# One eighth of the holographic attention of seven chunks is computed in the expert stage

## The chip, the cores and the metric

The kernel runs on one core of a Trainium2 chip. The metric is device microseconds (us) of one execution. The kernel before takes 1104.69 us (median of three runs, 1103.02 to 1106.05). A core has engines that run side by side, each through its own queue in order: PE (matrix products, results into PSUM), DVE (elementwise work, reductions, scans), ACT (elementwise functions), POOL (elementwise work), SP (here: issuing DMA transfers).

## The reference, cut to what matters

Two transformer-like layers over x of shape (16, 256, 128), float32. Every sublayer is x = x + gate * f(normalized and modulated x).

```python
x = x + ga * _L0_attn_ref(h, ...)       # layer 0: attention, 16 heads of 8
x = x + gb * _L0_ffn_ref(h, ...)        # layer 0: 16 experts, the best 4 of each token
x = x + ga * _L1_attn_ref(h, ...)       # layer 1: holographic attention
x = x + gb * _L1_ffn_ref(h, ...)        # layer 1: mixing of each token with the one before
```

The part that the change touches is the holographic attention; H * D = 16 * 64 = 1024 features:

```python
def _holo_fused_step(v, binder, probe):
    mem = jnp.cumsum(v * binder, axis=1)
    return jnp.real(mem * probe) / scale        # scale: sqrt(t + 1)
k = jnp.exp(1j * (k_real * PHASE_SCALE))
rotors = jnp.exp(1j * (t[:, None, None] * freqs))[None]
out_pos = _holo_fused_step(v, rotors, jnp.conj(rotors))
out_assoc = _holo_fused_step(v, jnp.conj(k_shifted), k)   # k_shifted: k one token later
out = out_pos * g_pos + out_assoc * g_assoc
return out.reshape(Bb, Tt, HD) @ Wo
```

So for every feature there are two running sums over the 256 tokens ("pos", bound by the rotor, and "assoc", bound by the phasor of the token before), each of a cosine and a sine; each sum is multiplied by its probe, and all go through Wo.

## The kernel before, in words

The 16 batch rows are worked on in 8 chunks of two rows (512 tokens). Three stages follow one another: the attention of layer 0; the expert stage; the holographic stage, which also holds the mixing of layer 1.

*Expert stage* (`for n in range(total + 4)`, 128 steps n = 16 c + e: chunk c, expert e). Step n: `gate_up(n)` has PE write pg (L752) and pup (L754), DVE add bias and limit into g (L756), ACT make u from pup (L758) and silu back into pg (L759), POOL clamp u (L760). `act(n - 1)` has DVE multiply u by pg (L766) and POOL by the scores of the expert (L767, tile `wide`). `down(n - 3)` has PE add the expert's product to the chunk's accumulator acc (L775; at e = 0 after a product with the biases b_dn, L774). pg has three PSUM banks, pup two, acc two; one bank (p_m) serves all else. `wide` comes by DMA, four experts (1 MB) at a time, into three buffers. At e = 2 ACT evicts the accumulator of the chunk before (chunk_end1, L784), at e = 3 it is transposed (pmo) and DVE adds it to x (L794); at e = 5 DVE takes the figures of the norm (L177, L178), at e = 7 POOL finishes them.

Side work is cut into small steps by generators, one step of each generator a step n: `last_end` (from n = 1) finishes layer 0's attention of the last batch row, and then lets `route` choose experts for the last five chunks (DVE, L261 to L285); its scores are due at n = 39. `prepare` (from n = 33) makes the modulation of layer 1, the rotor's angles and its sines (`turn_rotor`), scaled weights, the tokens of chunk 0 and, in `first_steps`, the values and phasors of the first two holographic parts and the bound values of the first.

*Holographic stage* (`for n in range(last + 2)`). The 1024 features are 8 parts of 128 (j), so 64 parts (c, j). Per part n: PE projects keys and values pk, pv of part n + 2 (L1035, L1039); DVE runs two scans of 128x1024 (cosine and sine, two rows of 256; `summed`, L1072): assoc into SBUF, pos into PSUM; `phases` (L1051, off) and the probe's product m_pos (L1298) are DVE's too; ACT makes the phasor (L1057 to L1059); POOL multiplies the assoc sums by their probe (L1303) and binds the values of part n + 1 twice (`binders`, L1069); PE takes four products of 512 columns through Wo (`out_project`, L1086). `keep` holds the scan's factors, 1 and 0 at the start of a row. At a chunk's end ACT scales by the gate (oT, L1099), PE transposes (pho), DVE adds to x (`into_stream`, L1112). The mixing of a finished chunk runs in later parts, placed by j: means, figures, power (POOL, L1161, L1162), norm, tokens, two pairs of products (pk2, pr2: `mixed`), values, gating, output. `tokens`, `turned` and `into_tokens` make the normalized tokens of the next chunk. Within the two stages the order on PE, DVE, ACT and POOL is as written.

## Time and profile before

| | us |
|---|---|
| median of three runs | 1104.69 |
| the profiled execution | 1106.3 |
| its span, first to last instruction | 1104.5 |
| attention of layer 0 | 0 to 306 |
| expert stage | 306 to 663.6 |
| holographic stage | 663.6 to 1083.2 |
| last chunk's ending | 1083.2 to 1104.5 |

Busy over the whole span: PE 1041.6, DVE 873.0, ACT 688.1, POOL 810.9. A stretch of the span has its own row of busy times, a group of instructions its mean duration (ns), and a row of the timeline its start and duration; what an engine waited for stands in square brackets behind the operation that it waited with. Spans of the same engine overlap by some hundredths of a microsecond, so that the spacing of starts is a little shorter than the durations.

### The profile page before, as it was taken

Reading aid. Unit: us, or ns where it says so; the run is one execution under the profiler, and the core shown is the slowest. Engines: PE = TensorE matmul, PEld = TensorE weight load, DVE = VectorE, ACT = ScalarE, POOL = GpSimd, SP = SyncE. Lnnn points to the kernel's source line nnn. Section 1 sums busy time; section 2 is a strip of 40 time slices with the busy share of each in tenths; the row PEclk is TensorE's granted clock in tenths of the full one; section 3 lists DMA queues with packets and bytes.
Section 4 is the critical chain, followed back from the end, with each engine's and each line's share of the span. In section 5 each row is a group of like instructions: output and inputs, shape, how many; then the busy total and the mean of one; then the engine's idle time right before and its main releaser. Section 6 shows DMA issues by size and latency. Waiting matters only on the chain.

```text
span 1104.5 us, 15892 instructions
## 1 busy us (share of the span) xinstructions
PE 1041.6 (94%) x5361; PEld 526.3 (48%) x5361; DVE 873.0 (79%) x1283; ACT 688.1 (62%) x1390; POOL 810.9 (73%) x720
## 2 busy tenths in 40 slices
PE   7999999999999999999999998889999999898987
PEld 5566766666644444444444443334443444343433
DVE  6678888997655877655555559999999999999994
ACT  3676767666655455555685445657767676867663
POOL 3245334542567677777776889999999999999992
PEclk8999999999999999999999999999999999999999
DMA  3102100000153223232222210000000000000000
GB/s 114 41 10 64 56 3 3 2 4 3 42 187 115 77 80 113 77 115 90 102 115 79 76 39 0 1 0 0 1 10 1 10 0 10 0 10 0 11 0 28
DMA packets 27200, 46.71 MB, mean 42 GB/s; under 512 B 7504, under 2 KB 22128, under 8 KB 23024
## 3 DMA queue, kind: packets, MB, share of 16 engines
q1 hardware_dynamic: 26576, 45.45, 11.9%
q8 instruction: 42, 0.69, 0.3%
q14 instruction: 38, 0.31, 0.1%
q10 hardware_dynamic: 544, 0.26, 0.1%
HBM read 43.07 MB, written 2.37 MB: 41 GB/s over the span
## 4 chain that ended last, share of the span: by engine, by line
PE 56%; DVE 23%; POOL 12%; issue 4%; ACT 3%; DMA 1%; SPq 0%; DVEq 0%; POOLq 0%; ACTq 0%
PE pg L752 9%; PE acc L775 9%; PE pup L754 9%; DVE sum_assoc L1072 7%; DVE mem L1072 7%; PE s L399 5%; PE po L453 5%; PE st L433 5%; DVE m_pos L1298 4%; POOL sum_assoc L1303 3%; POOL bound_assoc L1069 3%; POOL bound_pos L1069 3%; PE pout L1086 3%; PE pq L526 2%; DVE maxima L411 2%
## 5 line engine op out<-in xcount | busy, mean ns | idle before, releaser
L441 ACT ACTIVATE exp<-st 128x512 f32<-128x512 f32 x256 | 132.2, 602 | 88.2 <-PE st L433 88.2
L411 DVE TENSOR_REDUCE maxima<-s 128x2 f32<-128x512 f32 x256 | 158.9, 684 | 27.0 <-PE s L399 26.8
L767 POOL TENSOR_TENSOR u<-u,wide 128x512 f32<-128x512 f32 x128 | 163.1, 1275 | 19.3 <-DVE u L766 9.0
L756 DVE TENSOR_SCALAR g<-pg,b_gu 128x512 f32<-128x512 f32 x128 | 95.7, 747 | 103.2 <-PE pg L752 102.5
L758 ACT ACTIVATE u<-pup,b_gu 128x512 f32<-128x512 f32 x128 | 87.8, 686 | 138.0 <-PE pup L754 129.0
L1086 PE MATMUL pout<-m_pos,w_pos 128*128 128x512 f32 x256 | 128.7, 626 | 36.1 <-DVE m_pos L1298 28.9
L1072 DVE TENSOR_TENSOR_SCAN sum_assoc<-keep,bound_assoc 128x1024 f32<-128x1024 bf16 x64 | 146.0, 2282 | 4.6 <-POOL bound_assoc L1069 4.3
L1072 DVE TENSOR_TENSOR_SCAN mem<-keep,bound_pos 128x1024 f32<-128x1024 bf16 x64 | 145.4, 2272 | 0.0
L1303 POOL TENSOR_TENSOR sum_assoc<-sum_assoc,phasor 128x1024 f32<-128x1024 f32 x64 | 140.1, 2189 | 0.3 <-DVE sum_assoc L1072 0.3
L1069 POOL TENSOR_TENSOR bound_pos<-v,rotor 128x1024 f32<-128x1024 f32 x63 | 137.9, 2189 | 1.0 <-PE acc L775 1.0
L1069 POOL TENSOR_TENSOR bound_assoc<-v,phasor 128x1024 f32<-128x1024 f32 x63 | 138.0, 2191 | 0.0
L760 POOL TENSOR_SCALAR u<-u 128x512 f32<-128x512 f32 x128 | 81.6, 638 | 72.7 <-ACT u L758 69.2
L775 PE MATMUL acc<-u,w_dn 128*128 128x512 f32 x256 | 131.9, 597 | 2.9 <-POOL u L767 2.8
L752 PE MATMUL pg<-hT,w_gu 128*128 128x512 f32 x256 | 131.5, 595 | 1.6 <-DVE u L766 1.1
L754 PE MATMUL pup<-hT,w_gu 128*128 128x512 f32 x256 | 130.7, 592 | 0.0
L1086 PE MATMUL pout<-sum_assoc,w_assoc 128*128 128x512 f32 x256 | 120.7, 594 | 1.7 <-POOL sum_assoc L1303 1.7
L1086 PEld LDWEIGHTS pout<-m_pos,w_pos 128*128 128x128 f32 x256 | 45.3, 192 | 115.1 <-DVE m_pos L1298 66.5
L766 DVE SCALAR_TENSOR_TENSOR u<-u,pg 128x512 f32<-128x512 f32 x128 | 86.7, 678 | 8.2 <-POOL u L760 6.9
L759 ACT ACTIVATE pg<-g 128x512 f32<-128x512 f32 x128 | 75.9, 593 | 15.9 <-DVE g L756 15.8
L433 PE MATMUL st<-qx,kx 32*128 32x256 f32 x1024 | 82.3, 389 | 1.3 <-DMA qx<-turned 1.2
L1036 ACT ACTIVATE whole<-pk 128x512 f32<-128x512 f32 x62 | 36.9, 595 | 74.9 <-PE pk L1035 74.3
L399 PE MATMUL s<-kx,qx 32*128 32x256 f32 x1024 | 78.1, 409 | 4.1 <-DVE kx L536 1.8
(274 smaller groups left out, 1724.9 us busy)
## 6 DMA issues: line engine op xcount, KB each, us to landing
wide<-scores SPq DMA_DIRECT2D x32, 1024.0 KB
qx<-turned SPq DMA_DIRECT2D x256, 1.0 KB
w_gu<-in_gate_up_dram SPq DMA_DIRECT2D x8, 256.0 KB
out_dram<-x SPq DMA_DIRECT2D x16, 128.0 KB
x<-in_x_dram SPq DMA_DIRECT2D x14, 128.0 KB
w_dn<-in_down_dram SPq DMA_DIRECT2D x4, 256.0 KB
ga<-ga_rows SPq DMA_DIRECT2D x1, 768.0 KB
w_k<-in_Wk_dram SPq DMA_DIRECT2D x1, 512.0 KB
```

The costliest lines, as they stand in the source:

```text
L399: nc.tensor.matmul(s[g][:, i, :], qs[c][r][rows_, k, ts(i, P)], ks[c][rows_, r // NS, k, :], start=True, stop=True,)
L411: nc.vector.tensor_reduce(mx[:, :, g], s[g], AX.X, ALU.max, negate=True)
L433: nc.tensor.matmul(st[g][:, i, :], ks[c][rows_, r // NS, k, ts(i, P)], qs[c][r][rows_, k, :], start=True, stop=True,)
L441: nc.scalar.activation(e[:, g, :, :], st[g], AF.Exp, scale=QSCALE)
L752: nc.tensor.matmul(pg, w_gu[:, e, 0 : 2 * D : 2], h2, start=True, stop=True)
L754: nc.tensor.matmul(pu, w_gu[:, e, 1 : 2 * D : 2], h2, start=True, stop=True)
L767: nc.gpsimd.tensor_tensor(u, u, wide[n // SOME][:, n % SOME, :], ALU.mult)
L775: nc.tensor.matmul(accs[c], w_dn[:, e, :], work.pop(n), start=False, stop=(e == NE - 1))
L1069: nc.gpsimd.tensor_tensor(w[nm], v2, bind, ALU.mult)
L1072: nc.vector.tensor_tensor_scan(dst.rearrange("p s k t -> p (s k t)"), keep.rearrange("p s t -> p (s t)"), work[n][nm].rearrange("p s k t - ...
L1086: nc.tensor.matmul(pos[c], w[:, j, :], m[:, k, :, :].rearrange("p k t -> p (k t)"), start=(j == 0 and i == 0 and k == 0), stop=(j == NJ - ...
L1303: nc.gpsimd.tensor_tensor(m, m, phasor[(n - 1) % 3][:, :, :, 1:], ALU.mult)
```

## The change

Part j = 7 of chunks 0 to 6 leaves the holographic stage (`PARTS`: 7 parts for these chunks, 8 for chunk 7) and is computed by the generator `part_ahead(c)`, one step a step n of the expert stage from e = 8 of chunk c + 1. It makes the chunk's tokens (kept in the tile hT2 of that chunk), pv and pk of this part, and its phasor; then, one a step, eight pieces: two kinds (pos, assoc) of two rows and of cosine and sine, 128x256 each. POOL binds a piece, and a step later DVE reads it: a scan into a PSUM row, the product with probe and gate, and the addition to totals[c]. For chunk 6 there are two pieces a step. In the holographic stage totals[c] goes through one product of PE with w_last, the unscaled last rows of Wo, at j = 1.

Beside that: `prepare` starts at n = 1 in place of 33, with the angles of the last two parts first; `last_end` starts at n = 7 in place of 1; `wide` is loaded for two experts at a time; acc has one PSUM bank in place of two, the other goes to the PSUM row; and the places of the mixing are counted from the end of its chunk (2 to 13 parts later), not by j.

```diff
+AHEAD = NCH - 1
+PARTS = [NJ - 1 if c < AHEAD else NJ for c in range(NCH)]
...
-        SOME = 4
+        SOME = 2
...
-        lp = ctx.enter_context(tc.tile_pool(name="norm1", bufs=2, side="right"))
+        lp = ctx.enter_context(tc.tile_pool(name="norm1", bufs=1, side="right"))
...
+        w_last = load_late("w_last", [P, D], a["Wo"][HD - P :, :])
...
-                for nm, n in (("pe_g", 3), ("pe_u", 2), ("pe_acc", 2), ("pe_m", 1))
+                for nm, n in (("pe_g", 3), ("pe_u", 2), ("pe_acc", 1), ("pe_m", 1))
             )
+            p_sum = scope.enter_context(tc.tile_pool(name="pe_sum", bufs=1, space=bass.MemoryType.PSUM))
...
+            sums = p_sum.tile([P, 2, T], F32, tag="sum", name="sums")
+            nc.vector.memset(sums[:, 0, 0:1], 1.0)
+            keep_all, row = sums[:, 0, 0:1].to_broadcast([P, T]), sums[:, 1, :]
...
+                yield from angles(NJ // 2 - 1)
+                for h in range(2):
+                    nc.scalar.activation(w_k1[:, ts(h, 512)], w_k1[:, ts(h, 512)], AF.Copy, scale=PHASE / TWO_PI)
+                    yield
+                turn_rotor(NJ - 1)
+                yield
+                for p in range(NJ // 2 - 1):
+                    yield from angles(p)
...
-                for h in range(2):
-                    nc.scalar.activation(w_k1[:, ts(h, 512)], w_k1[:, ts(h, 512)], AF.Copy, scale=PHASE / TWO_PI)
-                    yield
...
-                tokens(0)
-                yield
-                pt = turned(0, hns.pop(0), p_m, "a1")
-                yield
-                into_tokens(0, pt)
-                for j in range(NJ):
-                    yield
+                for j in range(NJ - 1):
                     turn_rotor(j)
+                    yield
                 yield from first_steps()
...
+            def part_ahead(c):
+                j = NJ - 1
+                tokens(c)
+                yield
+                yield
+                into_tokens(c, turned(c, hns.pop(c), p_m, "a1"))
+                yield
+                flat = hTs[c].rearrange("p k t -> p (k t)")
+                v = cross.tile([P, 2, T], F32, tag="o", name=f"v_ahead_{c}")
+                pv = p_m.tile([P, 2, T], F32, tag="m", name=f"pv0_{c}")
+                nc.tensor.matmul(pv, w_v1[:, ts(j, P)], flat, start=True, stop=True)
+                nc.scalar.copy(v, pv)
+                bound = {}
+                def bind(nm, k, s, by):
+                    t = cross.tile([P, T], F32, tag=("heads", "y")[s], name=f"bound_ahead_{nm}_{c}_{k}_{s}")
+                    nc.gpsimd.tensor_tensor(t, v[:, k, :], by, ALU.mult)
+                    bound[nm, k, s] = t
+                def read(nm, k, s, i, probe):
+                    dst = totals[c][:, k, :]
+                    nc.vector.tensor_tensor_scan(row, keep_all, bound.pop((nm, k, s)), 0.0, ALU.mult, ALU.add)
+                    first = i == 0 and s == 0
+                    nc.vector.scalar_tensor_tensor(
+                        dst if first else row, row, gates[:, j, i : i + 1], probe, ALU.mult, ALU.mult
+                    )
+                    if not first:
+                        nc.vector.tensor_tensor(dst, row, dst, ALU.add)
+                cs = late.tile([P, 2, 2, T + 1], F32, tag="phasor_ahead", name=f"phasor_ahead_{c}")
+                nc.gpsimd.memset(cs[:, :, :, 0:1], 0.0)
+                pieces = [
+                    ("pos", k, s, 0, rotor[:, j, s, :], rotor[:, j, s, :]) for k in range(2) for s in range(2)
+                ] + [("assoc", k, s, 1, cs[:, s, k, 0:T], cs[:, s, k, 1:]) for k in range(2) for s in range(2)]
+                many = 2 if c == AHEAD - 1 else 1
+                def go(i):
+                    for q in pieces[max(i - 1, 0) * many : i * many]:
+                        read(*q[:4], q[5])
+                    for q in pieces[i * many : (i + 1) * many]:
+                        bind(*q[:3], q[4])
+                for i in range(8 // many + 1):
+                    yield
+                    if i == 0:
+                        pk = p_m.tile([P, 2, T], F32, tag="m", name=f"pk0_{c}")
+                        nc.tensor.matmul(pk, w_k1[:, ts(j, P)], flat, start=True, stop=True)
+                        off = cross.tile([P, 2, T], F32, tag="hn4", name=f"off_ahead_{c}")
+                        nc.scalar.activation(off, pk, AF.Copy, bias=ROUND)
+                        nc.vector.scalar_tensor_tensor(off, off, ROUND, pk, ALU.subtract, ALU.subtract)
+                    if i == 1:
+                        nc.scalar.activation(cs[:, 1, :, 1:], off, AF.Sin, scale=-TWO_PI_IN)
+                        nc.scalar.activation(off, off, AF.Abs)
+                        nc.scalar.activation(cs[:, 0, :, 1:], off, AF.Sin, bias=half_pi, scale=-TWO_PI_IN)
+                    go(i)
...
-                hTs[c] = lp.tile([P, 2, T], F32, tag="hT3", name=f"hT3_{c}")
+                hTs[c] = hT2[c]
...
+            totals = [late.tile([P, 2, T], F32, tag=f"total{c}", name=f"total{c}") for c in range(AHEAD)]
...
-            tasks.append([None, last_end(), 1])
-            def go_on():
-                for t in tasks[:1]:
-                    try:
-                        next(t[1])
-                    except StopIteration:
-                        tasks.remove(t)
+            last_steps = last_end()
...
                     widened(n // SOME + 2)
-                if n >= 1:
-                    go_on()
-                if n > 2 * NE:
+                if n > 6:
+                    next(last_steps, None)
+                if n > 0:
                     next(ready, None)
+                if e == 8 and 1 <= c <= AHEAD:
+                    ahead.append(part_ahead(c - 1))
+                for steps_ in ahead:
+                    next(steps_, None)
                 if n == total:
-                    assert next(ready, None) is None
+                    assert all(next(t, None) is None for t in [ready, last_steps, *ahead])
...
-        steps = [(c, j) for c in range(NCH) for j in range(NJ)]
+        steps = [(c, j) for c in range(NCH) for j in range(PARTS[c])]
...
                     start=(j == 0 and i == 0 and k == 0),
-                    stop=(j == NJ - 1 and i == (n < len(steps) - 1) and k == 1),
+                    stop=(j == PARTS[c] - 1 and i == (n < len(steps) - 1) and k == 1),
+                )
+            if i == 0 and j == 1 and c < AHEAD:
+                nc.tensor.matmul(
+                    pos[c], w_last, totals[c].rearrange("p k t -> p (k t)"), start=False, stop=False
                 )
...
+        begin = [sum(PARTS[:c]) for c in range(NCH)]
         for n in range(last + 2):
-            c, j = divmod(n, NJ)
-            now = c - 1 if 1 <= c <= NCH - 1 and j >= 2 else None
-            mixing = now is not None
-            gone = c - 2 if c >= 2 else None
+            c, j = steps[n] if n <= last else (NCH, 0)
+            place = {n - begin[m + 1]: m for m in (c - 2, c - 1) if 0 <= m < NCH - 1 and n <= last}
...
-            if mixing and j == 7:
-                mixed(now, wk_now, wk_before, "pk2")
-            if gone is not None and j == 0 and n < last:
-                mixed(gone, wr_now, wr_before, "pr2")
-            if gone is not None and j == 1:
-                mix_values(gone)
+            if 7 in place:
+                mixed(place[7], wk_now, wk_before, "pk2")
+            if 8 in place:
+                mixed(place[8], wr_now, wr_before, "pr2")
+            if 9 in place:
+                mix_values(place[9])
             if n + 2 <= last:
...
-            if j in (1, 2) and c:
-                into_stream(2 * (c - 1) + j - 1, pho[:, j - 1])
-            if j == 1 and c + 1 < NCH and n > 1 or n == 2:
+            if j == 1 and c:
+                for k in range(2):
+                    into_stream(2 * (c - 1) + k, pho[:, k])
+            if j == 1 and AHEAD <= c + 1 < NCH:
                 tokens(c + 1)
```

## The prediction

> **What bounds the kernel now.** I first cut the span into its stages, since the shares of the whole mix stages with different limits. Columns: stretch, its length, then busy time of PE, weight loads, DVE, ACT, POOL, then PE clock, DMA share, GB/s.
>
> ```profile
> 663.60:1083.20 419.60, 381.68 (x933) 163.92 (x934) 407.51 (x309) 279.17 (x584) 416.39 (x210) 0.99 0.01 4
> 306.00:663.60 357.60, 353.24 (x879) 159.50 (x879) 219.97 (x398) 199.71 (x366) 264.01 (x300) 1.00 0.26 95
> ```
>
> In the holographic stage (first line) POOL is full: 416.4 of 419.6 us, DVE close behind. In the expert stage PE is full: 353.2 of 357.6. The waits of POOL in the holographic stage confirm it; all of them are these (us, times, longest):
>
> ```profile
> POOL bound_pos L1069 <- PE acc L775: 1.0, 1, 1.0
> POOL sum_assoc L1303 <- DVE sum_assoc L1072: 0.3, 1, 0.3
> ```
>
> Then the timeline, for the spacing of operations. In steady holographic work POOL starts an operation every 2.13 to 2.14 us (941.26, 943.39, 945.53, 947.67), three a part, so 6.41 us a part. Last, DVE in the expert stage, where the router's choice for chunk 7 runs between the experts:
>
> ```profile
> 370.56 0.87 DVE L272 SCALAR_TENSOR_TENSOR rt_left<-rt_at,logits 128x320 f32<-128x320 f32 x1
> 371.35 0.74 DVE L756 TENSOR_SCALAR g<-pg,b_gu 128x512 f32<-128x512 f32 x1
> 372.02 0.67 DVE L766 SCALAR_TENSOR_TENSOR u<-u,pg 128x512 f32<-128x512 f32 x1
> 372.61 0.47 DVE L261 TENSOR_REDUCE rt_most<-rt_left 128x20 f32<-128x320 f32 x1
> 373.12 1.27 DVE L264 TENSOR_TENSOR rt_at<-rt_left,rt_most 128x320 f32<-128x320 f32 x1
> 374.42 0.78 DVE L265 TENSOR_TENSOR rt_at<-rt_at,ramp 128x320 f32<-128x320 f32 x1
> 375.12 0.74 DVE L756 TENSOR_SCALAR g<-pg,b_gu 128x512 f32<-128x512 f32 x1
> ...
> 376.51 1.13 PE L752 MATMUL pg<-hT,w_gu 128*128 128x512 f32 x2 [0.59 <-DVE u L766]
> ```
>
> An expert step lasts 2.58 us on PE (pg at 365.02, 367.59, 370.17: three products of 0.86). DVE's own share of it is 1.27 (0.67 from g to u, 0.60 on). Here g comes 4.0 us after it could (its pg began 370.17; undisturbed, g starts 0.96 after pg), and only then PE waits. Undisturbed, u of step n-3 is done 2.95 us before pg of step n needs its bank: DVE may run 2.95 us late at no cost. Where it is later, PE stalls by the rest.
>
> **The change, part by part.** The sum is made against the profiled execution: 1106.3 us, span 1104.5, 1.6 above the median of 1104.69.
>
> *Removed from the holographic stage:* 7 of 64 parts, hence 21 POOL operations of 2.137: **-44.9**. DVE loses 7 x 6.10 (2.20 + 2.18 scans, 0.59 off, 1.13 m_pos) = 42.7. Per chunk of seven, POOL then has 7 x 6.41 + 1.2 (the power of the mixing) = 46.1, DVE 42.7 + 2.6 (into_stream, mixing) = 45.3, PE 7 x 5.15 + 0.86 (w_last) + 4.3 + 1.8 = 43: POOL still sets the pace. The recount of the mixing puts pr2 (1.72) and w_last (0.86) into the same part j = 1, ahead of the next pk; off on DVE waits for that pk through ACT. At the part that began 831.23, pk's copy ended at 839.37 and DVE came to off at 839.55; with 0.86 more before it and 0.86 behind, less 0.60 for the second into_stream, DVE waits about 1 us, in five chunks. DVE's lead over POOL (scan ends 830.1, POOL uses it at 834.1; elsewhere 2.9) pays most of it. Bounds 0 (a wait gains nothing) and 5; I take **+2**, since the lead is 3 to 4.
>
> *Added to PE in the expert stage:* pk and pv of seven chunks, 14 x 0.86 = 12.0; transposes of six more chunks, 6 x 0.44 = 2.6 (362.00 to 362.44 for four). PE is full, so all shows: **+14.6**. Leaving the other stage, they give nothing back there, PE not being its bound.
>
> *Added to DVE:* per chunk eight scans of 128x256, eight products, six additions. No row has the scan at this size. Rows: 2282 ns for 1024, and additions of 1211 for 1024 (L1298) and 412 for 256 (L1195), so 145 ns fixed; that and a quarter of the rest gives 0.68, spacing 0.71, which I take. Bounds 0.57 (a quarter of 2282) and 0.9 (that plus one more fixed cost and a pointer's). The product with a pointer: 342 ns for 128 (L1112), so 0.48; the addition 0.41. Together 1.57 of spacing, 1.12 without the addition. With the 1.27 of the experts, 2.84 against 2.58: DVE falls behind 0.27 a step, at most 2.1 us in a chunk (with the figures, 1.6, at e = 5), below 2.95. **+0.6** in all for plain chunks, mostly at the single accumulator: its eviction ends about 4.1 us into step e = 2 and the next chunk's first product is due at 4.3.
>
> *The first chunk's part* starts at step 28 and now shares DVE with the router's choice (moved to steps 25 to 38 by the later start of last_end) and with the rotor angles (moved forward). Steps 25 to 38 on DVE: 14 x 1.27 = 17.8; router 19.5 (four rounds of 1.87 + 1.31 + 0.50, ends 4.8 with a 1.76 wait for Exp); part 11.6, off 0.6; angles 4.0; figures and stream 2.3: 55.8. PE in these steps: 14 x 2.58, pln, pv, pk, pmo, b_dn: 39.9. Less 2.95: PE stalls **13.0**. Bounds: 4.7 of the router's and angles' time is excess over the same rows' unblocked durations; without it and with scans of 0.57 it is 7.4, with twice the excess and scans of 0.9 it is 19.4. Before it, at step 17, figures wait for POOL's additions (2.7 us in the row) and make g 4 us late in the step ahead of the accumulator's eviction: b_dn waits **3.2** there. In return the old stalls go: 1.6 (PE on POOL's u) and 1.1 (on DVE's u) in the waits of this stage: **-2.7**.
>
> *Parts of chunks 2 and 3* meet first_steps: at step 65 DVE waits for pk1's copy with the part's reads behind it, 1.0; at steps 75 to 81 four bindings of 1.18 join the part's of 0.73 on POOL: 1.96 + 0.80 + 1.26 against 2.58, 4.95 behind at worst, of which 2.4 is free: 2.6. **+3.6**.
>
> *The end of the stage.* Chunk 6 reads two halves a step. From step 125 DVE needs 3.95, 3.95 and 4.39 a step; its u of step 127 is done 14.3 us after step 125 began, and two reads (3.1) stand behind it, ahead of keep and the first scan. Before:
>
> ```profile
> 662.21 0.69 DVE L766 SCALAR_TENSOR_TENSOR u<-u,pg 128x512 f32<-128x512 f32 x1 [1.00 <-POOL u L760]
> 663.73 2.30 DVE L1072 TENSOR_TENSOR_SCAN mem<-keep,bound_pos 128x1024 f32<-128x1024 bf16 x1
> ```
>
> The first scan starts 10.1 us after step 125 (653.65), after the change 18.1; POOL, which is bound from there, waits for the second scan and starts its first sum_assoc at 24.0 in place of 16.7: **+7.4**.
>
> *At nothing:* ACT gets 6.2 us a chunk more (norms 4 x 0.48, modulation 2 x 0.57, two copies, sines), with 157 us idle; no table load is added, since the Sines of first_steps show none beside Silu. SP issues 64 transfers of 512 KB for 32 of 1 MB, 0.32 us each; 1 MB took about 3 us (368 to 372), and from a buffer's release to its use there are 11 us even at four steps' notice; if they came late, POOL's product would wait step by step. POOL in plain chunks has 2.77 a step against 2.58, 1.5 behind at e = 3, 2.4 free.
>
> Sum: -44.9 + 2 + 14.6 + 0.6 + 13.0 + 3.2 - 2.7 + 3.6 + 7.4 = -3.2: 1103.1 beside 1106.3, **1101.5** beside the median.
>
> The row that speaks against this: rt_at took 1.27 us beside a POOL operation of 1.27 and 0.49 elsewhere. The Trainium skill (SBUF — State Buffer, "SBUF: two separate sides") says that a DVE operation with two SBUF inputs and a GpSimd one lock each other out for a whole instruction. The reads keep their row in PSUM and escape that, but 18 operations of router and angles don't; had each to wait for half a POOL operation, 11 us would stand where the rows hold 4.7, and the sum would end at 1108.
>
> **Rivals.** *Slower: the reads bind every chunk.* If one read is r longer than 1.57, a plain chunk stalls by 8r - 0.85; it decides from r = 0.1. For: no row shows this scan, and its three operations depend on one another. Against: m_pos follows a scan by 0.09 us at 666.12. At r = 0.3: five chunks x 1.55, 2.4 in the first, 2 at the end: +12, 1114.
> *Faster: the stalls are absorbed.* PE, stalled, gives DVE time that I count twice where stretches touch; the end's 7.4 falls to 3 if DVE reaches its last reads earlier than I have it, the first part's 13.0 to the bound of 7.4: 10 less, 1091.5. For: g was 4.0 late with 0.6 of stall. Against: the same lateness is reproduced by the sum of DVE's rows.
> *The holographic stage shrinks less:* PE at j = 1 has 8.2 against 6.4 and the lead is not rebuilt, 5 to 9 us lost: 1105 to 1109. Against: PE is idle 1.35 us a part.
>
> **Chances.** Forecast 0.50 (own range 1095 to 1108), slower rival 0.22, faster 0.20, third 0.08. Within 0.3% (1101.4 to 1108.0, about what can be told from no change) lie 0.17 of the forecast's half and 0.03 of the third; above, 0.06 of the forecast, 0.22, 0.05; below, 0.27 and 0.20. Range 1087 to 1115.
>
> **What would show it.** In the changed trace: the first m_pos to the last about 370 us (415.9 now) and POOL still without waits; steps 25 to 38 longer than PE's 39.9 by 10 us or more, PE's waits there naming DVE's u; the small scan at 0.68; first large scan some 4.4 us after the start of the last u (1.5 now). I am wrong if PE has no waits for DVE there, or if POOL waits in the holographic stage.

## The result and the profile after

The change makes the kernel slower: a median of 1122.59 us (five runs, 1118.91 to 1123.69) beside 1104.65 (five runs, 1103.02 to 1106.05), a ratio of 1.0157, interval 1.0136 to 1.0178. The forecast was 1101.5 with 1087 to 1115.

First the stages of the changed kernel, cut at the first gate product (pg) of the experts, at the first m_pos of the holographic stage and at its last. Columns: stretch, length, busy time of PE, weight loads, DVE, ACT, POOL, then PE's granted clock, DMA share, GB/s.

```profile
302.40:714.80 412.40, 384.37 (x938) 171.70 (x938) 308.98 (x560) 238.28 (x440) 301.90 (x366) 0.97 0.25 84
714.80:1094.70 379.90, 343.27 (x829) 147.64 (x830) 362.07 (x281) 240.27 (x511) 370.28 (x185) 0.99 0.02 5
```

The expert stage went from 359.8 us (306.3 to 666.1) to 412.4: **+52.6**, where the forecast's terms for it add up to +39.7. The holographic stage went from 415.9 to 379.9: **-36.0**, forecast -42.9. Both miss in the same direction and together by 19.8. The profiled run of the changed kernel is the fastest of its five, 3.7 us under their median, and no trace shows where the others lost more. Its attention stage ended 3.9 us earlier than in the profile before; in the traces shown here the first pg starts anywhere from 302.4 to 306.3 us, with the change or without. So the stages are compared by their own lengths.

PE was full in the expert stage before. Its waits in this stage now (what waits, for what: us in total, times, longest):

```profile
PE acc L784 <- ACT o L794: 10.2, 7, 3.5
PE pg L762 <- DVE u L776: 6.4, 5, 3.2
PE acc L785 <- POOL u L777: 4.9, 4, 2.8
PE psc L301 <- DVE scores L288: 3.3, 1, 3.3
```

The largest is the first product of each chunk (b_dn), which waits until ScalarE (ACT) has emptied the single accumulator: seven chunk ends, seven waits. Before the change PE's waits for DVE's u and for POOL's u came to 2.7 us up to 663.5.

In the holographic stage POOL, which had 1.3 us of waits, now has these, and DVE those of the third line (7.2 us in 8 waits before):

```profile
POOL bound_assoc L1136 <- ACT phasor L1126: 7.6, 6, 1.5
POOL bound_pos L1136 <- DVE sums L895: 1.4, 1, 1.4
...
DVE off L1118 <- ACT whole L1103: 15.7, 18, 2.2
```

Where they lie is seen from the distance of one m_pos to the next in a steady chunk, read from the starts on DVE:

| behind j = | 0 | 1 | 2 | 3 | 4 | 5 | 6 | 7 |
|---|---|---|---|---|---|---|---|---|
| before | 7.12 | 6.62 | 6.61 | 6.43 | 6.43 | 6.44 | 6.43 | 6.42 |
| changed | 7.12 | **8.16** | 6.78 | 6.43 | 6.43 | 6.43 | 6.43 | |

PE in the step of 8.16, one row for each group of matmuls (start, duration):

```profile
864.26 0.38 PE L1179 MATMUL pho<-ident,oT 128*128 128x128 f32 x2
864.48 1.88 PE L1153 MATMUL pout<-sum_assoc,w_assoc 128*128 128x512 f32 x4
866.19 1.02 PE L1201 MATMUL pr<-shifted,wr_now 128*128 128x512 f32 x2
867.05 1.02 PE L1202 MATMUL pr<-shifted,wr_before 128*128 128x512 f32 x2
867.91 1.88 PE L1153 MATMUL pout<-m_pos,w_pos 128*128 128x512 f32 x4
869.63 1.02 PE L1162 MATMUL pout<-total,w_last 128*128 128x512 f32 x2
870.49 1.02 PE L1102 MATMUL pk<-hT,w_k 128*128 128x512 f32 x2
```

No row has a wait: PE runs from start to start without a gap and reaches the next keys (pk) 6 us after the four transposes. Six products of 0.86 that every step has, two of pr2, one of w_last and 0.44 of transposes are 8.2 us, the length of the step. A steady chunk of the changed kernel takes 47.8 us (the sum of its row); POOL's own work in it is 46.1 by the prediction's rows. In the kernel before the sum is 52.5, which is POOL's work for eight parts by the same rows (8 x 6.41 + 1.2).

### The profile page after: what moved, and what is told of

Its sections match the earlier page's. It is cut to its first block, busy times and chain, and to the rows that moved or that the text cites. A ratio compares the mean times of both kernels' runs of the same rounds, so it can differ in the third digit from the quotient of the medians.

```text
span 1117.1 us, 16054 instructions
## 1 busy us (share of the span) xinstructions
PE 1031.3 (92%) x5319; PEld 520.7 (47%) x5319; DVE 917.7 (82%) x1417; ACT 687.6 (62%) x1390; POOL 802.6 (72%) x762
## 4 chain that ended last, share of the span: by engine, by line
PE 52%; DVE 28%; ACT 10%; issue 5%; POOL 3%; DMA 1%; SPq 0%; DVEq 0%; ACTq 0%; POOLq 0%
PE pg L762 7%; PE acc L785 7%; DVE sum_assoc L1139 6%; PE pup L764 6%; DVE mem L1139 6%; PE s L402 5%; PE st L436 5%; PE po L456 5%; PE pout L1153 4%; DVE m_pos L1370 4%; PE pq L529 2%; DVE g L766 1%; DVE maxima L414 1%; DVE sums L895 1%; DVE u L776 1%
## 5 line engine op out<-in xcount | busy, mean ns | idle before, releaser
L1153 PE MATMUL pout<-m_pos,w_pos 128*128 128x512 f32 x228 | 114.8, 627 | 34.9 <-DVE m_pos L1370 25.2
L1139 DVE TENSOR_TENSOR_SCAN sum_assoc<-keep,bound_assoc 128x1024 f32<-128x1024 bf16 x57 | 130.0, 2281 | 1.9 <-POOL bound_assoc L1136 1.9
L1139 DVE TENSOR_TENSOR_SCAN mem<-keep,bound_pos 128x1024 f32<-128x1024 bf16 x57 | 129.5, 2273 | 0.0
L1136 POOL TENSOR_TENSOR bound_assoc<-v,phasor 128x1024 f32<-128x1024 f32 x56 | 122.1, 2180 | 7.6 <-ACT phasor L1126 7.6
L1375 POOL TENSOR_TENSOR sum_assoc<-sum_assoc,phasor 128x1024 f32<-128x1024 f32 x57 | 124.3, 2182 | 0.7 <-DVE sum_assoc L1139 0.7
L1136 POOL TENSOR_TENSOR bound_pos<-v,rotor 128x1024 f32<-128x1024 f32 x56 | 122.2, 2182 | 2.0 <-DVE sums L895 1.4
L1153 PE MATMUL pout<-sum_assoc,w_assoc 128*128 128x512 f32 x228 | 107.5, 594 | 0.0
L1153 PEld LDWEIGHTS pout<-m_pos,w_pos 128*128 128x128 f32 x228 | 40.8, 194 | 104.7 <-DVE m_pos L1370 54.5
L1103 ACT ACTIVATE whole<-pk 128x512 f32<-128x512 f32 x55 | 32.7, 594 | 89.0 <-PE pk L1102 87.9
L785 PEld LDWEIGHTS acc<-u,w_dn 128*128 128x128 f32 x256 | 48.4, 193 | 71.6 <-issue 47.2
```

The source lines that it names most:

```text
L785: nc.tensor.matmul(accs[c], w_dn[:, e, :], work.pop(n), start=False, stop=(e == NE - 1))
L1136: nc.gpsimd.tensor_tensor(w[nm], v2, bind, ALU.mult)
L1139: nc.vector.tensor_tensor_scan(dst.rearrange("p s k t -> p (s k t)"), keep.rearrange("p s t -> p (s t)"), work[n][nm].rearrange("p s k t - ...
L1153: nc.tensor.matmul(pos[c], w[:, j, :], m[:, k, :, :].rearrange("p k t -> p (k t)"), start=(j == 0 and i == 0 and k == 0), stop=(j == PARTS ...
L1375: nc.gpsimd.tensor_tensor(m, m, phasor[(n - 1) % 3][:, :, :, 1:], ALU.mult)
```

## What the stages took in every run

All experiments in one table. Ratio: of the times, to the runs of the kernel before on the same chip, with its 95% interval. The stages are each from one trace. Experts: first pg to first m_pos. Holographic: first m_pos to last.

| run | ratio | experts, us | holographic, us |
|---|---|---|---|
| before | 1 | 359.8 | 415.9 |
| changed | 1.0157 [1.0136, 1.0178] | 412.4 | 379.9 |
| e1_one_acc (on before) | 0.9999 [0.9988, 1.0011] | 359.9 | 415.8 |
| e9_order_alone (on before) | 1.0023 [1.0012, 1.0035] | 363.2 | 415.7 |
| e10_dve_held (on before) | 1.0168 [1.0151, 1.0185] | 377.9 | 415.9 |
| x1_before_spread (on before) | 0.9997 [0.9987, 1.0006] | 359.9 | 416.0 |
| e2_last_at_4 | 1.0109 [1.0088, 1.0130] | 414.1 | 378.1 |
| e3_stream_two_steps | 1.0147 [1.0124, 1.0170] | 413.1 | 379.9 |
| e4_first_part_back | 1.0107 [1.0092, 1.0123] | 401.1 | 386.3 |
| e5_last_part_back | 1.0144 [1.0125, 1.0163] | 404.3 | 385.8 |
| e6_no_pieces | 0.9923 [0.9907, 0.9938] | 384.8 | 381.3 |
| z4_products_only | 0.9935 [0.9922, 0.9949] | 389.8 | 381.4 |
| e7_two_acc | 1.0485 [1.0467, 1.0502] | 450.1 | 380.3 |
| e13_two_acc_one_u | 1.0100 [1.0085, 1.0116] | 407.3 | 379.7 |
| y1_mixing_spread | 1.0061 [1.0045, 1.0078] | 411.8 | 370.8 |
| z1_spread_first_back | 0.9939 [0.9925, 0.9952] | 393.0 | 377.5 |
| z2_five_parts | 0.9910 [0.9896, 0.9924] | 382.3 | 384.1 |

Runs e2, e3 and y1 leave the expert stage as the change has it, and it took 414.1, 413.1 and 411.8 us in them, 412.4 in the changed kernel: a difference of 2 us between two traces is not clear of chance.

## The experiments

**The holographic stage.** First the added product of w_last is moved within the chunk:

```diff
-            if i == 0 and j == 1 and c < AHEAD:
+            if i == 0 and j == 4 and c < AHEAD:
```

> The changed kernel with the matmul of w_last and totals issued at j = 4 of a chunk in place of j = 1. In the changed kernel the distance from m_pos to m_pos behind j = 1 is 8.16 us in five chunks (6.62 before). Theory A (the added matmul, 0.86 us, delays the next keys, and with them DVE's phase offsets, in the step that already carries the sums into the stream): that step falls to 7.2 to 7.4 us, 4 to 6 us faster in all, about 1117. Theory B (the step is long because all four additions to the stream now lie in it): no change within 2 us.

The step behind j = 1 fell from 8.16 to 7.31 in every steady chunk, by the 0.85 of the product, and that behind j = 4 rose from 6.43 to 6.68: theory A for this step. The ratio is 0.5% lower; in the trace the stage gained only 1.8 us, as the second chunk's step behind j = 0 took 9.76 in place of 8.68. The ratio compares medians; the trace of the changed kernel is that of its fastest run.

```diff
-            if j == 1 and c:
-                for k in range(2):
-                    into_stream(2 * (c - 1) + k, pho[:, k])
+            if j in (1, 2) and c:
+                into_stream(2 * (c - 1) + j - 1, pho[:, j - 1])
```

> The changed kernel with the additions of a finished chunk to the stream split over j = 1 and j = 2 again, as in the kernel before. Theory B (two more additions of some 0.3 us each hold DVE up in j = 1): the step behind j = 1 falls from 8.16 to about 7.5 us, that behind j = 2 stays within 0.2 us of 6.78, 3 to 5 us faster, about 1118.5. Theory A (the added matmul): within 1 us of the changed kernel.

The step stayed at 8.16 and the stage at 379.9. DVE's additions are not the cause; that leaves PE's row of products.

If it is PE's, the cure is to spread PE's work over the steps. The mixing's products get a place of their own:

```diff
-                mixed(place[7], wk_now, wk_before, "pk2")
+                mixed(place[7], wk_now, wk_before, "pk2", whole=place[7] == NCH - 2)
             if 8 in place:
-                mixed(place[8], wr_now, wr_before, "pr2")
+                mixed_end(place[8], wk_before)
             if 9 in place:
-                mix_values(place[9])
+                mixed(place[9], wr_now, wr_before, "pr2", whole=False)
+            if 10 in place:
+                mixed_end(place[10], wr_before)
+            if 11 in place:
+                mix_values(place[11])
```

mixed with whole=False issues the first of its two products, mixed_end the second; the sigmoid moves to 11, the products with it to 12, the outputs to 13, w_last to j = 6.

> The changed kernel with the matmuls of the channel mixing spread: the two of pk2 in steps 7 and 8 of a chunk's count, the two of pr2 in 9 and 10, pv2 in 11, both products and the transposes in 12, both outputs in 13, and the matmul of w_last at j = 6. Theory A (what the holographic stage lost is PE's own work: in the step behind j = 1 lie the six matmuls of every step, two of pr2, that of w_last and four transposes, 8.2 us of PE): the steps of 7.12, 8.16 and 6.78 us fall to 6.4 to 6.7, the stretch from the first to the last m_pos from 379.9 to 364 to 370 us, the time to about 1110. Theory B (POOL or DVE sets these steps): the long steps stay or move to where the mixing goes, under 4 us faster.

The stage fell by 9.1 us to 370.8, the forecast's 370, and POOL's waits in it to 1.3 us, as many as before the change. The steps of DVE are now 7.12, 7.14, 6.09, 6.09, 6.09, 6.8 and 6.76. The long ones at a chunk's start did not go, against the expectation, but the sum is 46.1: POOL's own work. DVE is late by 1.4 us after two steps and makes up 1.0 of it in the next three, while POOL goes on. So a long step alone is no loss; one that is not made up within the chunk is. On the kernel before, where the sum is already POOL's, this says that nothing is to be had by spreading:

```diff
-                mixed(gone, wr_now, wr_before, "pr2")
+                mixed(gone, wr_now, wr_before, "pr2", whole=False)
             if gone is not None and j == 1:
+                mixed_end(gone, wr_before)
+            if gone is not None and j == 2:
                 mix_values(gone)
```

> The kernel before, no part ahead, with the second matmul of pr2 moved from j = 0 to j = 1 and the sigmoid and pv2 from j = 1 to j = 2. Theory A (PE's work in the step behind j = 0 makes it 7.12 us where the others take 6.43): that step falls to 6.4 to 6.6, 3 to 6 us faster than the kernel before, about 1100. Theory B (the step is long because ScalarE empties the chunk's sum there): within 1.5 us of the kernel before.

The step stays at 7.12 and the ratio is 0.9997. The result is theory B's, though not shown to be for its reason (ScalarE). Spreading the mixing is worth nothing by itself; it repairs what the change put into one step.

**The expert stage: one accumulator.** The largest wait in the trace names it, so it is put into the kernel before by itself:

```diff
-                for nm, n in (("pe_g", 3), ("pe_u", 2), ("pe_acc", 2), ("pe_m", 1))
+                for nm, n in (("pe_g", 3), ("pe_u", 2), ("pe_acc", 1), ("pe_m", 1))
```

> The kernel before with one PSUM accumulator in place of two, nothing else. Theory A (each chunk's first down matmul waits for ScalarE to empty the only accumulator, and this alone costs what the trace of the changed kernel shows, 10.2 us of PE waits at seven chunk ends): 8 to 12 us slower, about 1114. Theory B (the accumulator only costs where ScalarE is late because of the added parts; in the plain kernel its two copies of 0.46 us fit beside the two expert matmuls of 0.86 us that stand between): 0 to 3 us slower, about 1106.

No cost at all: theory B. The accumulator hurts only where ScalarE comes late, and one chunk end of the changed kernel shows what makes it late (from the timelines of DVE, ACT and PE, one after the other):

```profile
517.51 0.69 DVE L954 SCALAR_TENSOR_TENSOR whole<-whole,pk 128x512 f32<-128x512 f32 x1 [0.59 <-ACT whole L952]
518.12 0.69 DVE L895 TENSOR_TENSOR_SCAN sums<-sums,und_ahead_assoc 128x256 f32<-128x256 f32 x1
518.85 0.49 DVE L897 SCALAR_TENSOR_TENSOR sums<-sums,gates,phasor_ahead 128x256 f32<-128x256 f32 x1
519.38 0.42 DVE L901 TENSOR_TENSOR total<-sums,total 128x256 f32<-128x256 f32 x1
519.72 0.74 DVE L766 TENSOR_SCALAR g<-pg,b_gu 128x512 f32<-128x512 f32 x1
...
520.49 0.60 ACT L769 ACTIVATE pg<-g 128x512 f32<-128x512 f32 x1 [1.79 <-DVE g L766]
521.03 0.82 ACT L794 ACTIVATE o<-acc,gbT 128x256 f32<-128x256 f32 x2
...
521.90 1.12 PE L784 MATMUL acc<-scT,b_dn 16*128 16x512 f32 x2 [1.41 <-ACT o L794]
```

The read of the part ahead (518.12 to 519.7) stands in DVE's queue ahead of g; silu stands in ScalarE's queue ahead of the copies that empty the accumulator and waits 1.79 us for g; the copies come at 521.03 and PE stands 1.41 us. Of the 1.79 us that silu waits for DVE, 1.41 reach PE.

**What makes DVE late.** Left out are first the products and reads of every part, then the reads alone:

```diff
-                    go(i)
+                    if i == 0:
+                        nc.gpsimd.memset(totals[c], 0.0)
```

> The changed kernel with the eight products and the eight reads of each part ahead left out (the sums are set to zero): the output is not the reference's. PE's, ScalarE's and SyncE's work stays, and so do the accumulator and the order of the preparation. Theory A (DVE's reads make DVE late for the experts, and the stalls and the halved clock come from that): the expert stage falls by 22 to 32 us, time 1090 to 1100. Theory B (PE's added matmuls, the single accumulator and the moved preparation carry the cost): it falls by 4 to 12 us, time 1110 to 1118.

```diff
-                    for q in pieces[max(i - 1, 0) * many : i * many]:
-                        read(*q[:4], q[5])
...
+                nc.gpsimd.memset(totals[c], 0.0)
```

> The changed kernel with POOL's eight products of each part kept and DVE's eight reads left out (the sums are set to zero): the output is not the reference's. It splits the 27 us by which leaving out both shortened the expert stage. Theory A (DVE's own time in the reads makes it late): within 4 us of the run without both, about 1097. Theory B (the products hold POOL, which comes late for the experts' second factor and holds up DVE's operations with two operands in SBUF): 10 us or more above the run without both, 1106 or more.

Without both, the expert stage is 27.6 us shorter; with POOL's products back it is still 22.6 shorter. So the reads on DVE carry 22.6 and the products 5.0: theory A, in both. The smaller figure is the less certain: the medians of the two runs differ by 2.5 us, the ratios by 0.0012. In the run without both, b_dn waits at two chunk ends only (4.1 us). What it keeps is the moved work and the moved order; the order by itself was put into the kernel before:

```diff
-                if n >= 1:
-                    go_on()
-                if n > 2 * NE:
+                if n > 6:
+                    next(last_steps, None)
+                if n > 0:
                     next(ready, None)
```

> The kernel before with the preparation begun in step 1 in place of 33 and the last chunk's end of attention begun in step 7 in place of 1, as in the changed kernel; no part ahead. Theory A (the angles of the preparation then meet the router's choice on DVE, steps 20 to 40, and the scores of the last chunks come late, the 3.3 us that PE waits in step 39): 3 to 10 us slower than the kernel before, about 1111. Theory B (the order is harmless without the parts): within 2 us of the kernel before.

It costs 3.4 us of the expert stage and 0.23% in time, near theory A's lower end: PE waits 1.8 us for the scores of the last chunks and 2.4 us for DVE's u. So the 52.6 us split into 3.4 (order), 21.6 (384.8 - 363.2: PE's moved work with what hangs on it) and 27.6 (products and reads).

Where in the stage they lie is seen from the starts of b_dn, one a chunk: the time from one to the next, before them that from the first pg, and behind them that to the first m_pos (e4 and e5 follow below).

| from b_dn of chunk | first pg | 0 | 1 | 2 | 3 | 4 | 5 | 6 | 7 to first m_pos |
|---|---|---|---|---|---|---|---|---|---|
| before | 7.5 | 46.2 | 45.6 | 45.2 | 43.3 | 43.3 | 44.6 | 45.9 | 38.1 |
| e9_order_alone | 7.4 | 44.9 | 50.2 | 45.3 | 44.6 | 45.9 | 43.3 | 43.3 | 38.1 |
| e6_no_pieces | 7.4 | 47.2 | 53.2 | 50.7 | 47.8 | 47.2 | 45.5 | 45.5 | 40.3 |
| changed | 7.4 | 47.2 | 60.9 | 54.7 | 49.3 | 51.3 | 47.7 | 46.0 | 48.0 |
| e4_first_part_back | 7.4 | 47.2 | 54.5 | 49.8 | 49.3 | 51.2 | 47.6 | 46.0 | 48.0 |
| e5_last_part_back | 7.4 | 47.2 | 62.6 | 54.7 | 49.3 | 51.3 | 47.7 | 46.0 | 38.1 |

From e9 to e6 the undisturbed columns (5, 6 and the last) grow by 2.2 us each, the two added products and the transposes of one chunk (1.72 + 0.44). Over the stage these are 14.6 of the 21.6; the other 7.0 are the waits of b_dn at two chunk ends (4.1) and, by difference, what followed a fall of PE's clock behind the second (414 to 421 us).

**Where the reads cost most.** The part of the first chunk, which meets the router's choice, and that of the last, which does two pieces a step, each go back into the holographic stage:

```diff
-PARTS = [NJ - 1 if c < AHEAD else NJ for c in range(NCH)]
+PARTS = [NJ - 1 if 0 < c < AHEAD else NJ for c in range(NCH)]
...
+                if c == 0:
+                    return
```

> The changed kernel with the last part of chunk 0 done in the holographic stage again (its tokens are still made between the experts); chunks 1 to 6 as changed. The holographic stage gets one step longer, 6.7 to 7 us. Theory A (the first part meets the router's choice on DVE, steps 25 to 39, and the stalls of PE that follow also halve its granted clock): the expert stage loses 14 to 22 us, so 7 to 15 us faster, about 1112. Theory B (the cost lies in PE's added work and the accumulator, whatever the place): the expert stage loses 2 to 6 us, 1 to 5 us slower, about 1125.

```diff
-AHEAD = NCH - 1
+AHEAD = NCH - 2
...
-                many = 2 if c == AHEAD - 1 else 1
+                many = 2 if c == NCH - 2 else 1
```

> The changed kernel with the last part of chunk 6 done in the holographic stage again; chunks 0 to 5 as changed. Theory A (this part, two pieces a step behind the last experts, fills DVE from about 696 to 722 us and lets PE stand and its granted clock halve): the expert stage loses 9 to 15 us, the holographic stage gains 6.5 to 7.5 us, so 2 to 8 us faster than the changed kernel, about 1117.5. Theory B (the end is long because of ScalarE's last phasor and the projection figures whatever the part): the expert stage loses under 5 us, 2 to 5 us slower, about 1126.

By the stage the first part costs the experts 11.3 us, the last 8.1. The table shows that e5's trace is 1.7 longer in chunk 1, which its edit does not touch; in its own column, the last, the part costs 9.9. So the first lies below what theory A expected (14 to 22) and the last within it (9 to 15); both lie well above theory B. Each costs more than the 5.9 to 6.4 us by which its step lengthens the holographic stage. With their own two products on PE taken off (1.72 each; the last part's transposes too, 0.44), they hold 9.6 and 7.7 us of lateness. (Chunks 1 and 2 together took 115.0 to 117.9 us in the runs that do not touch them; by those the first part holds 9.0 to 11.9.) That leaves 27.6 - 9.6 - 7.7, some 10 us, for the five parts in plain chunks. Columns 3 to 6 alone are 8.3 us longer than without products and reads, and what PE does there says why: b_dn waits 1.41, 1.65, 0.41 and 0.41 us at their ends, and in 4 and 5 its clock falls.

**PE's clock.** Behind its waits PE does not always go on at full speed. To see this without the change, DVE is held in the kernel before:

```diff
+            held = late.tile([P, 256], F32, tag="held", name="held")
+            nc.vector.memset(held, 1.0)
+            blocks = {59: 8, 75: 14, 91: 20, 107: 28}
...
+                for _ in range(blocks.get(n, 0)):
+                    nc.vector.tensor_scalar(held, held, 1.0, None, ALU.mult)
```

> The kernel before with DVE held by 8, 14, 20 and 28 idle multiplications of one 128x256 tile at the ends of steps 59, 75, 91 and 107 of the experts, where it runs with two accumulators and no part ahead. If one takes 0.2 to 0.3 us the blocks are about 2, 3.5, 5 and 7 us. Theory A (PE stands for the block less a slack of about 3 us, and where it has stood about 3 us its granted clock falls to half for about 4 us, which costs 2 us more): no wait at the first, a short one without loss of clock at the second, and at the longest a wait of 3 to 4 us followed by matmuls of twice the length; 5 to 12 us slower, more than PE's waits add up to. Theory B (the clock is granted as it comes, whatever PE has done): the time lost is PE's waits, the clock stays at 1.0 behind each.

The blocks on DVE and the products of PE behind them:

```profile
473.88 4.18 DVE L1004 TENSOR_SCALAR held<-held 128x256 f32<-128x256 f32 x8
...
516.16 0.75 DVE L756 TENSOR_SCALAR g<-pg,b_gu 128x512 f32<-128x512 f32 x1 [1.23 <-PE pg L752]
...
517.43 6.15 DVE L1004 TENSOR_SCALAR held<-held 128x256 f32<-128x256 f32 x14
...
524.89 1.13 PE L752 MATMUL pg<-hT,w_gu 128*128 128x512 f32 x2 [1.90 <-DVE u L766]
...
563.38 8.12 DVE L1004 TENSOR_SCALAR held<-held 128x256 f32<-128x256 f32 x20
...
572.81 2.08 PE L752 MATMUL pg<-hT,w_gu 128*128 128x512 f32 x2 [3.87 <-DVE u L766]
...
617.10 10.74 DVE L1004 TENSOR_SCALAR held<-held 128x256 f32<-128x256 f32 x28
...
629.15 2.08 PE L752 MATMUL pg<-hT,w_gu 128*128 128x512 f32 x2 [6.49 <-DVE u L766]
```

Blocks of 4.18, 6.15, 8.12 and 10.74 us (longer than expected) gave waits of 0, 1.90, 3.87 and 6.49: the last three are the block less 4.25 us each time. Not all of the 4.25 is lateness that costs nothing: DVE would have been idle for part of it. The second block begins at 517.43; the g before it started at 516.16, so that the next, 2.58 us later, was due at 518.74. Of the 4.25 us, 1.31 are DVE's idle time, and 2.94 are how late its u may be in a plain step, which is the prediction's 2.95. Behind the two longer waits the pair of matmuls takes 2.08 us in place of 1.02 to 1.13. The clock (last but two) around the third:

```profile
568.00:570.00 2.00, 0.95 (x3) 0.12 (x1) 1.79 (x7) 0.00 (x0) 0.00 (x0) 1.00 0.00 0
...
572.00:574.00 2.00, 1.19 (x2) 0.67 (x3) 2.00 (x4) 1.77 (x5) 1.16 (x1) 0.50 0.00 0
...
576.00:578.00 2.00, 2.00 (x3) 0.67 (x2) 0.27 (x1) 1.54 (x4) 1.15 (x2) 0.50 0.87 356
...
580.00:582.00 2.00, 2.00 (x6) 0.98 (x5) 0.77 (x3) 1.68 (x4) 0.86 (x2) 1.00 0.00 0
```

The waits add up to 12.3 us, the expert stage lengthened by 18.1: 5.8 us more, with two spells of half clock. Chunk by chunk it is 3.1 and 2.2 us beyond the wait where a spell follows, and 0.3 where none does. Theory A holds, though not for the time in all, 5 to 12 us. In the changed kernel, in stretches of 2 us, the expert stage shows six such spells: behind the waits of 3.18 us (406.7), 3.46 (417.9), 3.26 (437.4), 1.41 (521.9), 1.65 (573.2) and 2.85 (711.1); the kernel before has none in this stage. Summed over each stretch times one less its clock, PE lost 11.5 us of full speed in them, which need not all show in the time, since PE is not always the last to come. Without products and reads it lost 3.4, with the order alone nothing. What one spell costs is seen from b_dn of chunk 4 to the next: this took 49.6 us in e3, where no spell followed the wait of 1.43 at its start, and 51.2 to 51.3 in the changed kernel, e2, e4, e5 and y1, where one followed the same wait (1.41 to 1.43): 1.6 us.

The Trainium skill (TensorE: Matmul & The Clock Gate, "Part 1: The HAM clock gate (the "warmup" mystery)") tells of half clock after at least one idle window of about 3.4 us, the window running free of the kernel. The waits above that length agree: behind 3.46, 3.87 and 6.49 us the clock fell each time. Those below it do not: it fell behind 1.41 and 1.65 us here and behind 1.10 in e13 (373.5), while behind 1.90 in the run above it stayed. One and the same wait can go either way. The 2.19 us for the first emptying of the accumulator was followed by no spell in the changed kernel (357.0) and by one in the run with chunk 0's part back (358.6, clock 0.5 from 360 to 362); the 3.18 us for DVE's u by one in the changed kernel (406.7) and by none in e2 (410.1). So a wait under the stated length can cost a spell, and its length alone does not decide. That the place in the window decides is what the page would make of it; no run here shows the window.

**A second accumulator.** The change gave the accumulator's second bank of PSUM to the running sums. To give it back, a bank is taken once from these sums, which go to SBUF in place of their products:

```diff
-                for nm, n in (("pe_g", 3), ("pe_u", 2), ("pe_acc", 1), ("pe_m", 1))
+                for nm, n in (("pe_g", 3), ("pe_u", 2), ("pe_acc", 2), ("pe_m", 1))
...
-                    nc.vector.tensor_tensor_scan(row, keep_all, bound.pop((nm, k, s)), 0.0, ALU.mult, ALU.add)
+                    row = bound.pop((nm, k, s))
+                    nc.vector.tensor_tensor_scan(row, keep_all, row, 0.0, ALU.mult, ALU.add)
```

> The changed kernel with two accumulators again; the bank comes from the bank of the running sums: each sum is taken in place in SBUF in the tile of its product, and the constant of the scan lies in SBUF too. Theory A (the waits for the emptied accumulator, 10.2 us by the trace, and the clock that falls behind the longest of them, are the price of one accumulator where ScalarE runs late): 6 to 14 us faster than the changed kernel, about 1112. Theory B (the waits only move to the next tile that comes late, and the reads, with two operands in SBUF now, take longer): within 3 us of the changed kernel, or slower.

Slower by 37.7 us in the expert stage. The waits for the accumulator are gone, and 29.0 us of PE's waits for DVE's u stand in their place. The read's three operations, changed kernel first (count, busy us, mean ns):

```profile
L895 DVE TENSOR_TENSOR_SCAN sums<-sums,und_ahead_assoc 128x256 f32<-128x256 f32 x28 | 19.3, 690 | 0.8 <-POOL und_ahead_assoc L890 0.7
...
L901 DVE TENSOR_TENSOR total<-sums,total 128x256 f32<-128x256 f32 x42 | 17.8, 425 | 1.4
...
L897 DVE SCALAR_TENSOR_TENSOR sums<-sums,gates,phasor_ahead 128x256 f32<-128x256 f32 x28 | 13.7, 489 | 0.9
```

and with the sums in SBUF:

```profile
L897 DVE SCALAR_TENSOR_TENSOR und_ahead_assoc<-und_ahead_assoc,gates,phasor_ahead 128x256 f32<-128x256 f32 x28 | 28.4, 1014 | 0.9
...
L895 DVE TENSOR_TENSOR_SCAN und_ahead_assoc<-one,und_ahead_assoc 128x256 f32<-128x256 f32 x28 | 25.2, 900 | 0.0
...
L901 DVE TENSOR_TENSOR total<-bound_ahead_pos,total 128x256 f32<-128x256 f32 x14 | 14.3, 1020 | 0.5
```

The same product takes 1014 ns for 489, the same addition 1020 for 425 (677 for the other half of them). The single times of that product run from 457 to 1319 ns with the sums in SBUF and from 371 to 494 in the changed kernel: the same operation on the same operands is slow at some times and not at others. That is what the lock between DVE and POOL that the prediction weighed would do, and its remark that the reads escape it by keeping their row in PSUM fits. So the run does not say what a second accumulator is worth by itself.

Once the bank comes from the up projections:

```diff
-                for nm, n in (("pe_g", 3), ("pe_u", 2), ("pe_acc", 1), ("pe_m", 1))
+                for nm, n in (("pe_g", 3), ("pe_u", 1), ("pe_acc", 2), ("pe_m", 1))
```

> The changed kernel with two accumulators and one bank in place of two for the up projections; the running sums keep their bank. Theory A (the waits for the emptied accumulator go, 10.2 us, and ScalarE takes each up projection in time, within the 1.7 us that PE has other work): 4 to 10 us faster than the changed kernel, about 1115. Theory B (what makes ScalarE late for the accumulator makes it late for the up projection too, 128 times over): within 2 us of the changed kernel, or slower.

The experts gain 5.1 us, the time 0.57%: theory A's range, but its reason only in part. PE's waits did not shrink in all: the 10.2 us are gone, and 7.8 for ScalarE's copy of the up projection and 3.7 more for DVE's u have come. By the columns of the table above the gain lies in 0 (44.9 for 47.2, the first wait of b_dn with nothing in its place) and in 4 (47.9 for 51.3), where the spell behind 521.9 and the wait of 1.65 at its end are gone. In all PE loses 7.5 us to the clock in place of 11.5.

**Together.** The first run has the mixing spread, chunk 0's part back and the two accumulators; the second also has chunk 6's part back, so that chunks 1 to 5 alone are done ahead:

> The changed kernel with the mixing spread, the part of chunk 0 back in the holographic stage, two accumulators and one bank for the up projections. If the gains found one by one add up (10.6, 5.6 and 6.3 us by the ratios) it takes about 1100, which is 0.4% under the kernel before. If the accumulator's gain was the same waiting for DVE that the first part causes, the gains overlap and it takes 1103 to 1107.

> As the run with the spread mixing, two accumulators and chunk 0's part back, with the part of chunk 6 back in the holographic stage too: five parts ahead, chunks 1 to 5, all in steps of the experts that share DVE with nothing but the experts and the preparation. If the last part's stretch still costs more than its step of the holographic stage saves, 1 to 3 us under the run with six parts, about 1098; if not, 1 to 4 us above it.

The gains add up (1098.33 us for the first version, about 1100 expected), and the second version, a little beyond what was expected of it, beats both kernels: 1095.04 us (1093.6 to 1096.75) beside 1104.86, ratio 0.9910 with 0.9896 to 0.9924. Its expert stage and its holographic stage:

```profile
304.10:686.40 382.30, 371.00 (x922) 163.85 (x922) 285.00 (x515) 228.82 (x422) 290.66 (x346) 1.00 0.26 90
686.40:1070.60 384.20, 352.30 (x856) 151.22 (x857) 373.55 (x287) 251.90 (x529) 383.24 (x194) 0.99 0.02 5
```

The clock is 1.00 over the whole expert stage, which is 30.1 us shorter than in the changed kernel, more than the 24.5 that the three edits to it gave one by one (11.3, 8.1, 5.1; 26.3 with the last part's 9.9): no stand above 1.9 us is left, and no spell of half clock. Against the run with the order alone, five parts cost the experts 19.1 us, 3.8 each, and relieve the holographic stage by 31.6.

## Why the prediction was wrong, step by step

- *Seven parts removed, -44.9.* Right: a step that nothing disturbs takes 6.43 us (6.41 taken), before and after.
- *Mixing and w_last at j = 1, +2 with bounds 0 and 5.* Here it failed first: 8.9 us. The text had both sums: 8.2 us of PE for that step in the third rival, and a lead of 3 to 4 us of DVE over POOL that was to pay. A lead pays once; the loss, 47.8 less 46.1, comes in each of five chunks and is not made up in the other steps, and the spread run, which keeps all the work, has the 46.1. The third rival, given 0.08 and 5 to 9 us, was this case, and its objection ("PE is idle 1.35 us a part") is a mean over steps. POOL got waits, which the text named as a sign of error.
- *PE's moved work, +14.6.* Right: 2.2 us a chunk, 14.6 in all. The run without products and reads, less the order, gives 21.6; the rest is the waits of b_dn (4.1, see below) and one spell of the clock.
- *The first chunk's part, +13.0 within 7.4 to 19.4.* The run with it taken back shows 9.6 beside its own products, and the order costs 3.4 without it. The mechanism is there: from 390 to 440 us DVE is busy 47.6 of 50 us, PE 36.9. That the size fits is in part luck. Steps 25 to 38 took 56.4 us (pg at 375.02 and 431.37) for the 39.9 of PE's work; 9.9 of the 16.4 more are waits, 6.4 for DVE's u as foretold and 3.5 for the accumulator, and most of the rest is half clock, which has no term. Behind them PE waits 3.3 for the scores.
- *Figures and b_dn at step 17 to 19, +3.2; the old stalls, -2.7.* The wait there is 2.19 us, and the old stalls are gone. Right in kind.
- *The end of the stage, +7.4.* The last part holds 7.7 us beside its PE work. The size is right, the path in part: PE stands 4.6 us for POOL's u, which comes behind DVE's, and its clock falls; the first scan starts 2.5 us after the last u begins (4.4 foretold, 1.5 before).
- *Plain chunks, +0.6, and +3.6 beside first_steps: DVE "at most 2.1 us" behind, "below 2.95".* This is the step of the expert stage that failed worst: 4.2 foretold, some 10 measured. The price of a read was right (0.69 + 0.49 + 0.425 = 1.60, taken 1.57), so the slower rival's condition, a longer read, was not what happened. The 2.95 was right too. But it is the slack of u towards pg. At a chunk's end another path leads from DVE to PE, g, silu, the copies, b_dn, and it has the 0.2 us that the text itself names (eviction done at 4.1, due at 4.3). DVE's lateness was held against the wrong one of the two.
- *No term for the clock.* Six spells, 11.5 us of PE's full speed, spread over the stretches of the other points. The profile before showed the means to see it: 0.99 in the stage where one spell lies (676 to 681 us).
- *At nothing: ACT, SP.* SP and the smaller transfers stayed harmless, 1.1 us of DVE's waits in all. ScalarE is not short of time, but its order carries DVE's lateness to the accumulator, so "with 157 us idle" was no cover.

The direction was lost by 6.9 us in the holographic stage, at j = 1, and by 12.9 in the expert stage: some 6 of these in the plain chunks, the rest from the first chunk's end to the first part's, with spells of the clock in both. The rule on DVE and POOL that the prediction weighed, with its sum of 1108, is not needed for this; how much of it the router's and the angles' operations paid was not measured.

## What to carry to other kernels

When work is moved into a stage whose engines have slack, look for the shortest path from the late engine to the full one, at each kind of place (inside a chunk and at its end), since a wait in the carrier's queue can leave 0.2 us where the usual path leaves 2.9. A mean of idle time says nothing for the one step into which several edits put their work: add up the engine's rows for that step, and spread them, before counting on a lead. Price each part by the place where it lands: five of seven, with the mixing spread and a second accumulator, gained 0.9%; all seven in the form of the change cost 1.6%.

## What was not expected of the hardware

- PE's granted clock fell to half for some 4 to 8 us behind waits as short as 1.10, 1.41 and 1.65 us, and in one run and not in another behind one and the same wait (1.43, 2.19 and 3.18 us). A spell cost 1.6 us in one stretch with and without it, 2.2 and 3.1 where DVE was held.
- The same DVE product of 128x256 beside a working POOL: 0.49 us with one operand in PSUM, 1.01 on average and up to 1.32 with both in SBUF.
- DVE could be held 4.25 us in a plain step, the same three times over, before PE stood; 1.3 of it was DVE's own idle time.
